# Deformable sampling in a two-layer network: the product with a tap's weights moved from one to two steps behind the tap's transposes

## The chip, the cores and the metric

The kernel runs on one core of one Trainium2 chip. What counts is the device time of one execution in microseconds (us). Three runs of the kernel before took 7668.76, 7659.78 and 7680.08 us; their median is 7668.76 us. A further execution was recorded by the hardware profiler; it took 8447.64 us, and its span, from the first to the last instruction of the program, is 8445.7 us.

## The reference, cut to what matters

The input x has the shape (2, 128, 64, 64): two images, 128 channels, 4096 positions. Two layers follow one another. Layer 0 has a deformable convolution and a mixture of experts (FFN), layer 1 a state-space mixer and another FFN. Only the deformable convolution is touched by the change. It has four branches with kernels of 1x1, 1x1, 3x3 and 7x7, so 1 + 1 + 9 + 49 = 60 taps. For each tap and position an offset and a mask are computed, the image is sampled at the shifted place by bilinear interpolation, and the samples are multiplied with the tap's weights and summed over the taps of the branch:

```python
def deform_conv(x, off_w, off_b, mod_w, mod_b, reg_w, k, pad):
    offset = conv2d(x, off_w, off_b, pad)
    mask = 2.0 * jax.nn.sigmoid(conv2d(x, mod_w, mod_b, pad))
    ...
    py = base_y + off[:, :, 0]
    px = base_x + off[:, :, 1]
    sampled = bilinear_sample(x, py, px) * mask[:, None]
    O = reg_w.shape[0]
    return jnp.einsum('bckhw,ock->bohw', sampled, reg_w.reshape(O, C, k * k))

def branch(x, off_w, off_b, mod_w, mod_b, reg_w, gng, gnb, k, pad):
    y = deform_conv(x, off_w, off_b, mod_w, mod_b, reg_w, k, pad)
    return jax.nn.relu(group_norm(y, gng, gnb))
```

`bilinear_sample` reads four corners around each place and adds them with their weights. Each branch gives 256 channels. The four branches and a fifth, pooled one are joined by a 1x1 convolution with a group norm, and the result is added to x.

## The kernel before, in words

Everything is in fp32. The positions of an image are cut into 8 groups (NG) of 512, that is 4 tiles (GT) of 128 positions. For the sampling, a table in DRAM holds, for each place of the padded image, the four corners' channels beside each other (512 numbers, 2 KB), so that one row fetches all that a sample needs.

`run` works in this order. It normalises image 0 and writes its table. It computes the offsets of the first group. Then it calls `sample` for the 8 groups of image 0, and after that for the 8 groups of image 1: 2 x 8 x 60 = 960 taps.

One tap in `sample` does the following. POOL issues four gathers (L548), one for each tile of 128 positions, into a buffer v of 128 x 4 x 512 numbers; the pool of v has six buffers. DVE multiplies the upper two corners with their weights (L559), and, for two tiles at a time, the lower two into a PSUM tile `low` (L564), and adds them (L565). PE then transposes the two remaining halves of each tile onto each other, eight transposes (L569), into a PSUM tile `pst`, of which there are two. That adds the last two addends and puts the channels on the partitions. ACT copies `pst` into the SBUF tile `st` (L578), of which there are two. PE multiplies the weights of the tap with `st`, once for each half of the 256 output channels (L597), into the two PSUM tiles `out`, which gather all taps of a branch; the profile counts four matmul passes for it.

That product isn't issued in its own tap. `self.late` holds it, and it is issued in the next step, behind the next tap's transposes and copy. So PE's order in the steady state is: transposes of tap k, product of tap k-1, then the side work of the step, then the transposes of tap k+1. `product` also does what hangs on it. When it was the last of ten taps of a chunk of weights, it puts the loading of a later chunk (`load_chunk`, L234, a DMA of 1280 KB on SP's queue) on a list, `self.pending`, to be issued some steps later. When it was the last tap of a branch, ACT copies both tiles `out` to `ys` (L611) and stores them to DRAM (L612), and the statistics of `ys` on DVE (bn_stats) go on the same list.

Each step ends with side work. `conv.step()` issues a piece of the offsets of later groups: seven products (L336), which the profile shows as fourteen matmul passes. `rest.step()`, twice a step and three times in the first group, takes a step of other generators: in image 0 the norm and table of image 1 and the constant matrices of the mixer; in image 1 the generator `after(0)`, which does the end of layer 0's convolution for image 0 (`finish`), its FFN and the convolutions of the mixer. `finish` needs the sums of all branches of its image in DRAM and their statistics. It begins with two DMAs of weights and then yields until `self.pending` is empty.

The order of work on each engine is the order in which these Python functions issue it (`manual_schedule`); nothing is rearranged. Semaphores are set by the framework, and a tile that has all its buffers in use makes the instruction that would write it wait.

After the sampling, `mixer.run` works through the scan of layer 1 for image 0, 256 units, with `after(1)` as side work at four or five steps a unit, and then for image 1. In it POOL does the multiplications `db` (L1239) for the scan, and in the FFN of layer 0 the multiplications `gb` (L806). The FFN of layer 1 comes last.

Of the kernel before, what the change touches and what calls it, by code (L numbers as in the profile page):

```python
# [9 lines left out]
F32 = mybir.dt.float32  # L10
# [8 lines left out]
P = 128  # L19
# [9 lines left out]
NG = NT // GT  # L29
BRANCH = [(1, 0), (1, 0), (3, 1), (7, 3)]  # L30
TAPS = [(j, ky, kx, p) for j, (k, p) in enumerate(BRANCH) for ky in range(k) for kx in range(k)]
NTAP = len(TAPS)
# [139 lines left out]
def together(gens, n):  # L172
    for _ in mixed(gens, n):
        pass


class L0Conv:
# [281 lines left out]
    def run(self, build, after):  # L459

        env, tc, nc = self.env, self.env.tc, self.env.nc
        pools = lambda ctx: lambda name, bufs, **kw: ctx.enter_context(tc.tile_pool(name=name, bufs=bufs, **kw))
        with ExitStack() as ctx:
            pool = pools(ctx)
            self.rp, self.regw = pool("l0rw", 1), {}
            self.ip = pool("l0i", 2)
            self.vp = pool("l0v", 6)
            self.stp = pool("l0s", 2)
            self.pending = []
            first = ctx.enter_context(ExitStack())  # L470
            self.open_offsets(pools(first))
            for i in range(2):
                nc.vector.memset(self.padc[i], 0.0)
            self.zero_table(0)
            with (
                tc.tile_pool(name="nrm", bufs=3) as sp,
                tc.tile_pool(name="nrmp", bufs=4, space=PSUM) as pp,
            ):
                together([self.norm_group(0, g, sp, pp, "nrm") for g in range(NG)], 3)
            self.load_weights()  # L480
            self.zero_table(1)
            for _ in self.norm_end(0):
                pass
            self.p_w = pool("l0pw", 1, space=PSUM)
            self.p_r = pool("l0pr", 1, space=PSUM)
            self.p_t = pool("l0pt", 2, space=PSUM)
            self.p_o = pool("l0py", 2, space=PSUM)
            psum = ctx.enter_context(ExitStack())
            self.p_f = deque([pools(psum)("l0po", 1, space=PSUM)])
            early = psum.enter_context(ExitStack())  # L490
            p_m = pools(early)("l0pm", 1, space=PSUM)

            def more():

                early.close()
                self.p_f.append(pools(psum)("l0po2", 1, space=PSUM))
                yield

            cur = self.new_group(self.ip)
            for _ in self.offset_stream([(0, 0, cur)]):  # L500
                pass

            conv, rest = Side(), Side()
            self.late = None
            rest.add(self.norm(1, p_m, "misc"), more(), build)
            ahead = {}

            def runs():
                for g in range(1, NG):
                    ahead[g] = self.new_group(self.ip)  # L510
                    yield 0, g, ahead[g]
                    yield 1, g - 1, None
                yield 1, NG - 1, None

            conv.add(self.offset_stream(runs()))
            for g in range(NG):
                self.sample(0, g, *cur, conv, rest, 2 if g else 3)
                cur = ahead.get(g + 1)
            conv.drain()
            rest.drain()  # L520
            psum.close()
            first.close()
            side = ctx.enter_context(tc.tile_pool(name="l0ps", bufs=2, space=PSUM))
            rest.add(after(0, side))
            cur = self.load_group(1, 0)
            for g in range(NG):
                nxt = self.load_group(1, g + 1) if g + 1 < NG else None
                self.sample(1, g, *cur, conv, rest, 2 if g else 3)
                cur = nxt
            self.late()  # L530
            for _, f in self.pending:
                f()
            self.pending = []
            rest.drain()

    def sample(self, b, g, idx, w4, conv, rest, pace):

        env, nc = self.env, self.env.nc
        pw = None
        for br, (k, _) in enumerate(BRANCH):  # L540
            for t in range(FIRST[br], FIRST[br] + k * k):
                tw = t % HT
                if tw == 0:
                    pw = self.p_w.tile([P, GT, HT, 4], F32, name="pw")
                    nc.vector.tensor_copy(pw, w4[:, :, t : t + HT, :])
                v = self.vp.tile([P, GT, 4 * C], F32, name="v")
                for j in range(GT):
                    nc.gpsimd.indirect_dma_start(  # L548
                        out=v[:, j, :],
                        out_offset=None,  # L550
                        in_=self.table[b],
                        in_offset=bass.IndirectOffsetOnAxis(ap=idx[:, j, t : t + 1], axis=0),
                    )
                v4 = v.rearrange("p j (q c) -> p j q c", q=4)


                up = v4[:, :, 0:2, :]
                w = pw[:, :, tw, 0:2].unsqueeze(3).to_broadcast([P, GT, 2, C])
                nc.vector.tensor_tensor(up, up, w, ALU.mult)  # L559
                for j in range(0, GT, 2):  # L560
                    two = slice(j, j + 2)
                    low = self.p_r.tile([P, 2, 2, C], F32, name="low")
                    w = pw[:, two, tw, 2:4].unsqueeze(3).to_broadcast([P, 2, 2, C])
                    nc.vector.tensor_tensor(low, v4[:, two, 2:4, :], w, ALU.mult)  # L564
                    nc.vector.tensor_tensor(up[:, two], up[:, two], low, ALU.add)  # L565
                pt = self.p_t.tile([P, GT, P], F32, name="pst")
                for j in range(GT):
                    for q in range(2):
                        nc.tensor.matmul(  # L569
                            pt[:, j, :],  # L570
                            v4[:, j, q, :],
                            env.ident,
                            is_transpose=True,
                            start=j == 0 and q == 0,
                            stop=j == GT - 1 and q == 1,
                        )
                st = self.stp.tile([P, 512], F32, name="st")
                nc.scalar.copy(st, pt.rearrange("p j t -> p (j t)"))  # L578
                if self.late:
                    self.late()  # L580
                self.late = functools.partial(self.product, b, g, br, t, st)
                due = [f for n, f in self.pending if n == 0]
                self.pending = [(n - 1, f) for n, f in self.pending if n]
                for f in due:
                    f()
                conv.step()
                for _ in range(pace):
                    rest.step()

    def product(self, b, g, br, t, st):  # L590

        nc = self.env.nc
        first, last = t == FIRST[br], t == FIRST[br] + BRANCH[br][0] ** 2 - 1
        if first:
            self.out = [self.p_o.tile([P, 512], F32, name="out") for _ in range(2)]
        for half in range(2):
            nc.tensor.matmul(  # L597
                self.out[half],
                self.regw[t // CH][:, t % CH, half * P : (half + 1) * P],
                st,  # L600
                start=first,
                stop=last,
            )
        c = t // CH
        if t % CH == CH - 1 and c in (0, 1, 3, 4) and not (b == B - 1 and g == NG - 1 and c > 2):
            self.pending.append((4, functools.partial(self.load_chunk, c + 3 if c < 3 else c - 3)))
        if last:
            for half in range(2):
                r = 2 * br + half
                ys = self.stp.tile([P, 512], F32, name="ys", bufs=4)  # L610
                nc.scalar.copy(ys, self.out[half])  # L611
                nc.scalar.dma_start(out=self.yd[b][r, :, g * 512 : (g + 1) * 512], in_=ys)  # L612
                self.pending.append((4, functools.partial(nc.vector.bn_stats, self.stats[b][:, r, g, :], ys)))

    def finish(self, b, fp, sp, pp, cs):
# [8 lines left out]
        nc.sync.dma_start(out=pw, in_=d["pool_w"])  # L624
        mv = fp.tile([P, 10, 2], F32, name="mv")

        for _ in range(2):
            yield
        while self.pending:
            yield  # L630
        for i in range(8):
            nc.vector.bn_aggr(mv[:, i, :], stats[:, i, :, :])
# [1001 lines left out]
```

## Time and profile before

| | |
|---|---|
| median of three runs | 7668.76 us (7659.78 to 7680.08) |
| the profiled execution | 8447.64 us |
| its span | 8445.7 us |
| first and last gather (L548) | 199.0 and 6010.5 us |
| first and last product of the sampling (L597) | 241.0 and 6025.7 us |
| granted TensorE clock, mean of the span | 0.798 |
| DMA, mean over the span | 186 GB/s |

The profiled execution is longer than the timed ones by 778.88 us, so its durations can't simply be set against the median. In a row of the page's groups, the numbers before the bar say how often the group ran; behind it stand its busy time in us, the mean of one in ns, and the idle time of its engine just before it, with what ended the largest part of that. "remote" means that a semaphore ended the wait for which the profile could name no instruction. In a timeline row the first number is the start, the second the duration, both in us, and the brackets hold the idle time of the engine before it. The rows on PE come in two kinds: PE are matmuls, PEld the loading of weights ahead of them. The ends of matmuls are modelled by the profiler.

### The profile page before, as it was taken

The page shows a single profiled execution, that of the slowest core. Times are in us where ns is not written, and L with a number is a line of the kernel's source. Part 1 is how long each engine was busy: PE and PEld are TensorE (multiplying, and loading weights), DVE is VectorE, ACT ScalarE, POOL GpSimd, SP SyncE. Part 2 cuts the span into 40 slices and gives each one's busy share as a digit, 9 for nine tenths or more (in the row PEclk, how much of TensorE's full clock was granted, in tenths as well). Part 3 has the DMA queues.
Part 4 walks back from the last instruction along what each step waited for, and adds up shares of the span by engine and source line. Part 5 has one row for each costly group of instructions (what it writes and reads, how often), then busy time and mean ns, then how long its engine had stood idle before and what let it go on. Part 6 is the DMA issues. An engine that isn't in the chain of part 4 may idle for free. (4 is left out here: it accounts for less than half of the span.)

```text
span 8445.7 us, 85253 instructions
## 1 busy us (share of the span) xinstructions
PE 5931.0 (70%) x28533; PEld 4163.4 (49%) x28533; DVE 5703.1 (68%) x8472; ACT 2111.4 (25%) x4445; POOL 4585.4 (54%) x4556
## 2 busy tenths in 40 slices
PE   2688888888888867677667675667555666645569
PEld 2456566666666634344334443445344555523359
DVE  1577777777777776788876667667557636679950
ACT  1111111111111114111112111212353444555520
POOL 0456666666666666666665666666534323367610
PEclk9789999999999989888878887888776656656555
DMA  4676666666666678777677777777553334333333
GB/s 126 187 256 209 203 200 212 197 211 198 203 213 193 214 220 270 248 233 238 219 233 203 214 227 214 214 213 207 165 170 120 118 88 132 94 120 135 123 96 120
DMA packets 655029, 1574.34 MB, mean 186 GB/s; under 512 B 167768, under 2 KB 280192, under 8 KB 642052
## 3 DMA queue, kind: packets, MB, share of 16 engines
q0 software_dynamic: 307200, 1006.88, 39.8%
q1 hardware_dynamic: 284452, 494.19, 18.4%
q10 hardware_dynamic: 62944, 67.83, 2.3%
q8 instruction: 232, 3.80, 0.2%
q14 instruction: 201, 1.65, 0.1%
HBM read 1450.99 MB, written 120.01 MB: 186 GB/s over the span
## 5 line engine op out<-in xcount | busy, mean ns | idle before, releaser
L548 POOL DMA_INDIRECT v<-table,idx x3840 | 3643.1, 949 | 2367.9 <-issue 990.9
L597 PE MATMUL out<-st,regw 128*128 128x512 f32 x3840 | 2191.6, 700 | 704.2 <-issue 356.4
L559 DVE TENSOR_TENSOR v<-v,pw 128x1024 f32<-128x1024 f32 x960 | 1169.2, 1218 | 1069.9 <-DMA v<-table,idx 911.7
L578 ACT COPY st<-pst 128x512 f32<-128x512 f32 x960 | 557.6, 585 | 4338.7 <-remote 2312.1
L569 PE MATMUL pst<-ident,v 128*128 128x128 f32 x7680 | 1175.2, 296 | 389.3 <-issue 303.5
L597 PEld LDWEIGHTS out<-st,regw 128*128 128x128 f32 x3840 | 765.2, 222 | 1364.5 <-issue 980.4
L565 DVE TENSOR_TENSOR v<-v,low 128x512 f32<-128x512 f32 x1920 | 1318.0, 686 | 67.0 <-issue 1.7
L564 DVE TENSOR_TENSOR low<-v,pw 128x512 f32<-128x512 f32 x1920 | 1328.8, 692 | 34.1 <-DVE v L565 0.7
L569 PEld LDWEIGHTS pst<-ident,v 128*128 128x128 f32 x7680 | 976.4, 153 | 699.6 <-issue 569.0
L1239 POOL TENSOR_TENSOR db<-du,bcb 128x512 f32<-128x512 f32 x512 | 659.7, 1293 | 942.0 <-DVE da L1289 864.7
L336 PEld LDWEIGHTS po<-wout,ring 128*128 128x128 f32 x5120 | 732.6, 198 | 285.5 <-issue 284.5
L336 PE MATMUL po<-wout,ring 128*128 128x147 f32 x5120 | 757.3, 296 | 102.3 <-issue 99.0
L1289 DVE TENSOR_TENSOR_SCAN da<-da,state,db 128x512 f32<-128x512 f32 x512 | 656.9, 1283 | 245.3 <-ACT state L1296 211.4
L1262 PE MATMUL py<-ident,sc 128*128 128x128 f32 x2048 | 480.1, 389 | 374.5 <-DVE sc L1295 374.2
L1262 PEld LDWEIGHTS py<-ident,sc 128*128 128x128 f32 x2048 | 349.7, 201 | 523.2 <-DVE sc L1295 483.1
L1295 DVE TENSOR_TENSOR sc<-da,bcb 128x512 f32<-128x512 f32 x512 | 354.2, 692 | 88.5 <-PE py L1262 42.2
L1246 ACT ACTIVATE da<-delta,w_A_log 128x512 f32<-128x512 f32 x512 | 352.2, 688 | 15.9 <-DVE delta L1209 3.1
L972 PEld LDWEIGHTS ps<-tm,X 120*88 120x88 f32 x2048 | 249.3, 220 | 81.2 <-ACT Y L924 42.0
L972 PE MATMUL ps<-tm,X 120*88 120x48 f32 x2048 | 252.4, 304 | 52.2 <-ACT Y L924 25.8
L1296 ACT COPY state<-da 128x1 f32<-128x1 f32 x512 | 80.4, 157 | 544.6 <-DVE sc L1295 544.0
L988 PE MATMUL ps<-ident,Y 88*64 88x88 f32 x768 | 107.0, 287 | 151.8 <-ACT img L924 92.6
L959 PE MATMUL ps<-ident,hs 64*120 64x64 f32 x1408 | 141.8, 275 | 87.2 <-ACT X L924 75.5
(268 smaller groups left out, 5103.1 us busy)
## 6 DMA issues: line engine op xcount, KB each, us to landing
bcb<-bc SPq DMA_DIRECT2D x256, 512.0 KB
regw<-in_regw SPq DMA_DIRECT2D x66, 1280.0 KB
v<-table,idx POOLq DMA_INDIRECT x3840
yd<-ys ACTq DMA_DIRECT2D x128, 256.0 KB
yc<-yd SPq DMA_DIRECT2D x32, 1024.0 KB
gb<-gd SPq DMA_DIRECT2D x16, 2048.0 KB
tm<-pos SPq DMA_DIRECT2D x16, 1440.0 KB
table<-xn SPq DMA_DIRECT2D x128, 128.0 KB
```

The costliest lines, as they stand in the source:

```text
L336: m()
L548: nc.gpsimd.indirect_dma_start(out=v[:, j, :], out_offset=None, in_=self.table[b], in_offset=bass.IndirectOffsetOnAxis(ap=idx[:, j, t : t ...
L559: nc.vector.tensor_tensor(up, up, w, ALU.mult)
L564: nc.vector.tensor_tensor(low, v4[:, two, 2:4, :], w, ALU.mult)
L565: nc.vector.tensor_tensor(up[:, two], up[:, two], low, ALU.add)
L569: nc.tensor.matmul(pt[:, j, :], v4[:, j, q, :], env.ident, is_transpose=True, start=j == 0 and q == 0, stop=j == GT - 1 and q == 1,)
L578: nc.scalar.copy(st, pt.rearrange("p j t -> p (j t)"))
L597: nc.tensor.matmul(self.out[half], self.regw[t // CH][:, t % CH, half * P : (half + 1) * P], st, start=first, stop=last,)
L972: nc.tensor.matmul(ps[:, c, :], X[:, c0 + c, :], tm[:, :, c0 + c], start=True, stop=True)
L1239: nc.gpsimd.tensor_tensor(dbs[u], pieces[k]["du"][:, half, :], bcb[u // 2][:, 0, :], ALU.mult)
L1262: nc.tensor.matmul(out[:, j, :], what[:, j * P : (j + 1) * P], env.ident, is_transpose=True, start=first and j == 0, stop=last and j == GT ...
L1289: nc.vector.tensor_tensor_scan(s, s, dbs.pop(u), state[:, half, n : n + 1], ALU.mult, ALU.add)
```

## The change

The single delayed product becomes a queue of delayed products. Each step appends its own product, and when more than two wait, the oldest is issued. In the steady state the product of tap k-2 is thus issued behind the transposes of tap k. The tile `st` has three buffers instead of two, since the copies of three taps can be alive at a time. At the end of image 1, whatever is left in the queue is issued. `product` counts the products issued for each image in `self.made`. `finish` yields until all 480 products of its image were issued and `self.pending` is empty, instead of yielding twice and then until the list is empty.

```diff
@@ run
             conv, rest = Side(), Side()
-            self.late = None
+            self.late, self.made = deque(), [0, 0]
@@ run, behind the last tap
-            self.late()
+            for f in self.late:
+                f()
@@ sample
-                st = self.stp.tile([P, 512], F32, name="st")
+                st = self.stp.tile([P, 512], F32, name="st", bufs=3)
                 nc.scalar.copy(st, pt.rearrange("p j t -> p (j t)"))
-                if self.late:
-                    self.late()
-                self.late = functools.partial(self.product, b, g, br, t, st)
+                self.late.append(functools.partial(self.product, b, g, br, t, st))
+                if len(self.late) > 2:
+                    self.late.popleft()()
@@ product
         nc = self.env.nc
+        self.made[b] += 1
@@ finish
-        for _ in range(2):
-            yield
-        while self.pending:
+        while self.made[b] < NG * NTAP or self.pending:
             yield
```

The lines of the code behind the change move: the transposes are L570, the copy L579 and the product L599 in the changed kernel, the gathers L549.

## The prediction

> **What bounds the kernel now.** I read the page first: its span, its engine totals and its groups.
>
> ```profile
> span 8445.7 us, 85253 instructions
> ...
> PE 5931.0 (70%) x28533; PEld 4163.4 (49%) x28533; DVE 5703.1 (68%) x8472; ACT 2111.4 (25%) x4445; POOL 4585.4 (54%) x4556
> ...
> L548 POOL DMA_INDIRECT v<-table,idx x3840 | 3643.1, 949 | 2367.9 <-issue 990.9
> L597 PE MATMUL out<-st,regw 128*128 128x512 f32 x3840 | 2191.6, 700 | 704.2 <-issue 356.4
> ...
> L578 ACT COPY st<-pst 128x512 f32<-128x512 f32 x960 | 557.6, 585 | 4338.7 <-remote 2312.1
> ```
>
> No engine is full over the span, so the stage must be taken alone. The rows of tile v put the first gather at 199.0 us and the last at 6010.5: 5811.5 us for 960 taps, 6.05 each, 69% of the span. The other 30% (the mixer and the last FFN) is touched only at one seam.
>
> In this stage POOL issues four gathers a tap. The timeline spaces them 1.25 us apart when nothing holds them (0.95 busy, 0.30 issue), so POOL alone needs 3643.1 + 3840 x 0.30 = 4795 us. The remaining 1017 us are waits of POOL. The windows of L548 show 212 gathers in the first 600 us: 600 - 199 - 212 x 1.25 = 136 us of the waits lie there. The other 881 spread over 907 taps, 0.97 each. The waits say for whom:
>
> ```profile
> POOL v L548 <- issue: 990.9, 3244, 0.6
> POOL v L548 <- remote: 458.5, 187, 4.7
> POOL v L548 <- PE pst L569: 391.8, 162, 12.4
> ```
>
> "issue" is the floor above; the two other rows are POOL waiting for a buffer v, which the transposes L569 free. The timeline shows why the transposes are late (PE and ACT rows):
>
> ```profile
> 1514.57 1.04 PE L569 MATMUL pst<-ident,v 128*128 128x128 f32 x8
> 1515.44 1.88 PE L597 MATMUL out<-st,regw 128*128 128x512 f32 x4
> 1517.16 1.93 PE L336 MATMUL po<-wout,ring 128*128 128x147 f32 x14
> 1518.93 1.03 PE L569 MATMUL pst<-ident,v 128*128 128x128 f32 x8
> 1519.80 1.88 PE L597 MATMUL out<-st,regw 128*128 128x512 f32 x4
> 1521.52 1.93 PE L336 MATMUL po<-wout,ring 128*128 128x147 f32 x14
> 1523.28 0.98 PE L569 MATMUL pst<-ident,v 128*128 128x128 f32 x5
> 1524.70 0.54 PE L569 MATMUL pst<-ident,v 128*128 128x128 f32 x3 [0.44 <-issue]
> ...
> 1526.24 0.58 ACT L578 COPY st<-pst 128x512 f32<-128x512 f32 x1 [8.13 <-PE pst L569]
> 1526.43 0.94 POOL L548 DMA_INDIRECT v<-table,idx  x1 [1.85 <-PE pst L569]
> ...
> 1526.88 1.99 PE L597 MATMUL out<-st,regw 128*128 128x512 f32 x4 [1.64 <-issue]
> ```
>
> Unhindered, PE needs 4.36 us a tap for the first image (1514.57 to 1518.93), less than POOL's 5.0. But the product of 1526.88 needs the copy of 1526.24, the copy of the transposes that ended at 1519.96. That copy came 6.3 us after them, ACT idle before it. PE stood 1.64 us, and POOL was released in the same moment. So PE, which has the work of 4.36 us, is held by a copy that is late, and POOL by PE.
>
> **The profiled execution is not the timed one.** It took 8447.64 us (1.94 around its span), the median of the runs is 7668.76: 778.88 less. If head (199) and tail (8445.7 - 6010.5 = 2435) cost the same in both, the gathers take 7668.76 - 199 - 2435 - 2 = 5033 us there, 238 above POOL's 4795. Most of the 1017 us of waits would then not exist when nothing is recorded. This decides the forecast.
>
> [...] granted clock 0.50 from 1501 to 1507, 1.00 from 1508 to 1524, 0.91 over 600 to 3100 and 0.84 over 3100 to 6030. [...]
>
> **The change, part by part.**
> - *Product two taps behind.* PE's row becomes: transposes of tap k, product of k-2, offset matmuls or side steps. No instruction is added or removed. Between the end of tap k's transposes and the first instruction that needs its copy lay, unhindered, 1515.61 to 1519.80 = 4.2 us (its product). Now that first instruction is the transposes of k+2, since pst keeps two buffers: 1515.61 to 1523.28 = 7.7 us. The wait moves from the product to these transposes; behind it stand that tap's product and side matmuls, and DVE and ACT wait for the latter. The copy needed there is one tap older than the one that stopped PE before, so no transpose waits longer than now. Cost zero, gain from zero up to all waits behind a late copy.
> - *Third st.* The copy of k must find the product of k-3 done; with two buffers and the old order it was k-2. Either stands before tap k's transposes on PE: 0. It adds 2 KB a partition.
> - *Drain of the queue.* The last two products run after the last tap, four passes of 0.43 us instead of none: +1.7 us. At the first image's end two products run inside the second image, hidden under POOL's 5.0 us a tap.
> - *One tap later:* ys copies with their yd DMAs on ACT's queue, bn_stats on DVE, and load_chunk with its DMA on SP's queue (past up to three side steps' DMAs). A chunk still is asked for five taps after its predecessor's last product and needed some 15 taps (75 us) later: 0. Uncovered, it would hold a product and one tap, 5 us, 66 times.
> - *finish waits for a count.* For the first image it starts about one tap (two or three side steps) later. Its chain ends before the sampling does (no side row stands in 6009 to 6026 of the timeline): 0. For the second image the two empty yields fall away, so its chain moves two steps forward against the mixer's scan, which takes four or five steps a unit. POOL's order there changes: gb (L806, 8 x 4.73 us) meets other neighbours.
>
> The sum on the profiled execution: from 0 to -881 us (+1.7). On the timed one the gather stage has only 238 us above its floor. If the first 600 us keep their 136 (the norm of the second image shares the DMA queues there, and DVE waits for landings), 102 are left. I take half of them, since side chains also hold DVE (19.4 us at 5017.95, for xst), where a later product helps nothing: **-50 us, 7620**. Both ends: 0, and 238 as long as a gather costs 1.25.
>
> **Rivals.**
> - *Modest gain, as worked out: 7620, own range 7555 to 7646. Chance 0.45.* For it: PE's waits before L597, 704 us, the largest of its groups. Against: the copy may not be late at all without the recorder.
> - *No change: 7669, within 23 us. 0.20.* POOL already runs at 5.03 to 5.24 us a tap in the timed runs, and the six v buffers (six taps, 30 us) swallow what PE loses. For it: the 778.88 us.
> - *Large gain: 7420. 0.20.* The recorder slows everything alike (7668.76 / 8447.64 = 0.908). The gathers then take 5276 of a floor of 4353, so 923 us of waits are real; a quarter to a third of them gone is -250. For it: POOL waits much alike in both images, by the windows of L548 0.89 us a tap over 600 to 3100 and 1.06 over 3100 to 6030. Against: the gathers' 0.95 us is so even that I doubt that recording lengthens it.
> - *Slower: 7715. 0.15.* The seam in the mixer: with the second image's chain two steps earlier, gb comes to stand before the multiplications db (L1239) at points where the scan has no lead. Lead is three units, 1987 / 512 x 3 = 11.6 us; a db behind two xs or zc (1.3 to 2.2 each) and two gb (9.5) is past it. Eight gb wholly exposed are 38 us; I take 46, for what then waits on ACT and PE behind them. For it: POOL idles 864.7 us for da there, so the scan is a strict alternation; against: the same idle time is its slack.
>
> **How the numbers follow.** A measurement of this kernel tells about 0.3% (23 us) from no change. Faster: 0.45 + 0.20 = 0.65; same 0.20; slower 0.15. The likeliest case gives 7620. The range leaves out the lower half of the large gain (0.10, below 7420) and two thirds of the slower case (0.10, above 7710): 7420 to 7710.
>
> **What would show it.** Right: in the changed kernel's trace the group L599 has far less than 704 us of idle before it, part of it back before L570 with ACT st as releaser; the granted clock over 600 to 3100 above 0.91; POOL's waits for pst and "remote" below 850 together, the gathers still 1.25 apart. Wrong in size: if the profiled span falls by hundreds of us while the timed runs fall by 50 or less, the recorder had made the lateness; if the timed runs fall by more than 238, a gather costs less than 1.25 unrecorded or my head and tail do. Wrong in place: if the copies come as late as before, now one tap further on (about 7.7 us after the transposes), the signal was waiting for PE to stop, and no distance helps. Slower: the stretch after the last gather over 2435 us.

## The result, and the profile after

The changed kernel takes 7717.85 us (median of 6 runs, 7709.35 to 7738.3) where the kernel before takes 7672.42 (6 runs beside it, 7659.78 to 7681.92): ratio 1.0063, 95% interval 1.0046 to 1.008. It is slower by some 45 us, and the forecast was 7620. One thing is needed to read the numbers: the second batch of experiments (e5 to e8) ran on a chip on which the kernel before takes about 8385 us, where others take 7651 to 7672, so every experiment is compared with the kernel before on its own chip. The execution that was profiled first, of 8447.64 us, resembles those of that chip; whether it ran there isn't known. In the text TensorE is PE, VectorE DVE, ScalarE ACT, GpSimd POOL and SyncE SP.

The page of the changed kernel, with the lines that answer to those shown of before:

```profile
span 7707.6 us, 85112 instructions
...
PE 5671.2 (74%) x28533; PEld 3994.3 (52%) x28533; DVE 5681.0 (74%) x8472; ACT 2121.9 (28%) x4441; POOL 4593.8 (60%) x4556
...
L549 POOL DMA_INDIRECT v<-table,idx x3840 | 3651.1, 951 | 1588.3 <-issue 937.2
L599 PE MATMUL out<-st,regw 128*128 128x512 f32 x3840 | 1994.9, 646 | 51.6 <-ACT ys L613 51.6
L579 ACT COPY st<-pst 128x512 f32<-128x512 f32 x960 | 562.4, 586 | 3500.7 <-PE pst L570 3470.5
...
L1295 DVE TENSOR_TENSOR sc<-da,bcb 128x512 f32<-128x512 f32 x512 | 354.2, 692 | 112.6 <-PE py L1262 65.2
```

The idle time before the product (L599) is 51.6 us, and the profiled execution is 738 us shorter than that of before. Read against the first profile, this looks like the gain that was forecast. It is not. The kernel before, profiled once more (the run `e3_before_again`, 7657.45 us), has the same lines without the change:

```profile
span 7655.5 us, 85253 instructions
...
L548 POOL DMA_INDIRECT v<-table,idx x3840 | 3641.8, 948 | 1582.3 <-issue 928.6
L597 PE MATMUL out<-st,regw 128*128 128x512 f32 x3840 | 1989.8, 644 | 55.4 <-ACT ys L611 53.5
...
L1295 DVE TENSOR_TENSOR sc<-da,bcb 128x512 f32<-128x512 f32 x512 | 354.2, 692 | 85.9 <-PE py L1262 39.4
```

Its product waited 55.4 us, not 704.2. POOL's waits are alike too. First the changed kernel, then the kernel before, in the view of waits (us in total, times, longest):

```profile
POOL v L549 <- issue: 937.2, 3068, 1.6
POOL v L549 <- PE pst L570: 178.2, 103, 7.7
POOL v L549 <- DMA v<-table,idx: 127.3, 309, 4.2
```

```profile
POOL v L548 <- issue: 928.6, 3047, 0.6
POOL v L548 <- PE pst L569: 170.4, 103, 7.5
POOL v L548 <- DMA v<-table,idx: 135.8, 333, 5.8
```

The timeline of the kernel before shows a tap as it is where nothing is late (rows of PE and ACT, two taps):

```profile
1516.39 1.04 PE L569 MATMUL pst<-ident,v 128*128 128x128 f32 x8
1517.26 1.88 PE L597 MATMUL out<-st,regw 128*128 128x512 f32 x4
1517.52 0.58 ACT L578 COPY st<-pst 128x512 f32<-128x512 f32 x1 [3.77 <-PE pst L569]
...
1518.98 1.93 PE L336 MATMUL po<-wout,ring 128*128 128x147 f32 x14
...
1520.74 1.03 PE L569 MATMUL pst<-ident,v 128*128 128x128 f32 x8
...
1521.62 1.88 PE L597 MATMUL out<-st,regw 128*128 128x512 f32 x4
```

The copy starts at 1517.52, 0.09 us after the transposes end, and is done at 1518.10, 3.5 us before its product at 1521.62. The median over all 960 taps is the same 0.09 us, so a product one tap behind has its operand in time already. The 6.3 us that the prediction read between the transposes and a copy are therefore no distance that belongs to the program.

From the starts of the gathers, taps 60 to 540 take 5.035 us each in both: 599.6 to 3016.3 us in the changed kernel, 606.4 to 3023.2 in the kernel before. The difference of the spans, 52.1 us, lies elsewhere: 17.3 us at the end of the last product (5252.6 against 5235.3) and 34.8 us in the stretch from there to the end, here called the tail (2455.0 against 2420.2). Of the 17.3, the taps 540 to 660 alone lose 22.4 (675.6 against 653.2 us); 6.8 were gained ahead of tap 60. Each of these stretches is read from one recorded execution, and the tails of kernels with all gathers and the side chain of before range from 2412 to 2423 us. So there are two places, and in neither is the product concerned.

### The profile page after: what moved, and what is told of

Its sections match the earlier page's. It is cut to its first block, busy times and chain, and to the rows that moved or that the text cites. A ratio compares the mean times of both kernels' runs of the same rounds, so it can differ in the third digit from the quotient of the medians.

```text
span 7707.6 us, 85112 instructions
## 1 busy us (share of the span) xinstructions
PE 5671.2 (74%) x28533; PEld 3994.3 (52%) x28533; DVE 5681.0 (74%) x8472; ACT 2121.9 (28%) x4441; POOL 4593.8 (60%) x4556
## 5 line engine op out<-in xcount | busy, mean ns | idle before, releaser
L549 POOL DMA_INDIRECT v<-table,idx x3840 | 3651.1, 951 | 1588.3 <-issue 937.2
L599 PE MATMUL out<-st,regw 128*128 128x512 f32 x3840 | 1994.9, 646 | 51.6 <-ACT ys L613 51.6
L570 PE MATMUL pst<-ident,v 128*128 128x128 f32 x7680 | 1201.1, 293 | 743.3 <-issue 420.2
L579 ACT COPY st<-pst 128x512 f32<-128x512 f32 x960 | 562.4, 586 | 3500.7 <-PE pst L570 3470.5
L570 PEld LDWEIGHTS pst<-ident,v 128*128 128x128 f32 x7680 | 918.0, 149 | 1149.3 <-issue 674.6
L599 PEld LDWEIGHTS out<-st,regw 128*128 128x128 f32 x3840 | 722.6, 209 | 586.1 <-issue 520.6
L336 PEld LDWEIGHTS po<-wout,ring 128*128 128x128 f32 x5120 | 693.0, 190 | 150.6 <-issue 150.6
L336 PE MATMUL po<-wout,ring 128*128 128x147 f32 x5120 | 706.5, 288 | 0.0
L972 PEld LDWEIGHTS ps<-tm,X 120*88 120x88 f32 x2048 | 246.9, 216 | 62.1 <-issue 37.3
L675 PE MATMUL pfo<-yc,fw 128*128 128x256 f32 x512 | 149.4, 442 | 56.4 <-ACT yc L677 56.4
```

What stands on the lines that cost most here:

```text
L336: m()
L549: nc.gpsimd.indirect_dma_start(out=v[:, j, :], out_offset=None, in_=self.table[b], in_offset=bass.IndirectOffsetOnAxis(ap=idx[:, j, t : t ...
L570: nc.tensor.matmul(pt[:, j, :], v4[:, j, q, :], env.ident, is_transpose=True, start=j == 0 and q == 0, stop=j == GT - 1 and q == 1,)
L599: nc.tensor.matmul(self.out[half], self.regw[t // CH][:, t % CH, half * P : (half + 1) * P], st, start=first, stop=last,)
L972: nc.tensor.matmul(ps[:, c, :], X[:, c0 + c, :], tm[:, :, c0 + c], start=True, stop=True)
```

## The experiments

Two things happen at these places. From about tap 490 on the first image's finish runs as side steps, and in taps 540 to 660 the feed-forward that follows it (FFN; its multiplications gb fall in taps 561 to 645). The change starts this side chain one tap later, since the last product, its statistics and the count come one tap later. In the mixer the second image's finish starts two side steps sooner, since two empty yields were dropped.

**Which part costs.** First the two yields put back into the changed kernel, and the same two taken out of the kernel before, for the second image alone:

```diff
 changed kernel, finish (e1)
+        for _ in range(2):
+            yield
         while self.made[b] < NG * NTAP or self.pending:
 kernel before, finish (e2)
-        for _ in range(2):
+        for _ in range(0 if b else 2):
             yield
```

> The changed kernel with the two empty yields put back in front of the wait in finish, so that the second image's side chain meets the mixer's scan where it did before; queue, third st and count stay. Seam theory (the loss lies in the mixer, because the chain starts two side steps earlier): the stretch from the last product to the end goes back from 2455 to about 2419 us, and the time to 7665 to 7690. Queue theory (the loss lies in the sampling): the stretch may move, the time stays at 7705 to 7735.

> The kernel before with nothing changed but the two empty yields in finish, left out for the second image. Seam theory: 7700 to 7725, 30 to 50 us slower than before, with ACT waiting some 16 times for pfo in the mixer. Queue theory: within 10 us of before.

Measured: with the yields back 7671.17 against 7653.56, ratio 1.0023 (1.0013 to 1.0033); the tail is 2422.1. The kernel before without them: 7697.7, ratio 1.0067 (1.0051 to 1.0082); tail 2461.0. Two empty yields, which issue nothing, are worth more than 40 us, and without any later product. What remains of the change costs 0.0023: a share of the time of the kernel before, as all such figures below, about 18 us.

The kernel before once more, and with a third buffer for st alone, first in a single run and then timed:

```diff
-                st = self.stp.tile([P, 512], F32, name="st")
+                st = self.stp.tile([P, 512], F32, name="st", bufs=3)
```

> The kernel before, profiled a second time. If the late copies belong to this program under the recorder, its profiled span is again near 8446 us, copies 3 to 8 us behind their transposes. If the first profile was an accident, the span is near 7670 and copies follow within 0.1 us.

> The kernel before with three buffers of st and nothing else. If the third buffer removes the late copies from the profile, its span is near 7670; if the order on PE does, near 8446 as before. The time without a profile stays within 15 us of before under either.

> The kernel before with a third buffer for the copied samples and nothing else, timed. If a copy sometimes waits for the product of two taps earlier, the single look (7646) stands: ratio 0.998 to 0.9995. If the buffer is never waited for, 0.9995 to 1.0005.

The first gave the profile shown above: the late copies don't belong to the program. The buffer gave 7646.36 in the single run and a ratio of 1.0009 (0.9999 to 1.0018) when timed: above both ranges expected, but no effect that can be told from none.

**The remaining 0.0023: the later product, or the side chain that it shifts?** One run keeps the later product and lets the deferred statistics and chunk loads fall due one tap earlier, so that VectorE, GpSimd and SyncE issue exactly what the kernel before issues; the other has the kernel before and only shifts the first image's side chain by a tap.

```diff
 changed kernel with its two yields back, product (e5)
-                self.pending.append((4, functools.partial(nc.vector.bn_stats, ...)))
+                self.pending.append((3, functools.partial(nc.vector.bn_stats, ...)))
 (the same 3 for load_chunk)
 kernel before, finish (e6)
         while self.pending:
             yield
+        for _ in range(0 if b else 3):
+            yield
```

> The changed kernel with the two empty yields back and with the deferred statistics due after 3 taps instead of 4, so that VectorE, GpSimd and SyncE issue exactly what they issue in the kernel before, in the same order; only the product and the copies of finished sums stand one tap later on TensorE and ScalarE. Theory A (what is left of the loss, about 17 us of 7653, comes from the side chain of the first image, which starts one tap later): ratio 0.999 to 1.001, taps 540 to 660 at the pace of the kernel before (5.35 and 5.54 us a tap). Theory B (the later product itself costs it, by standing in TensorE's queue ahead of side work): ratio 1.002 as with the yields alone, taps 540 to 600 at 5.5 us or more.

> The kernel before, with three yields after the finish's wait for the first image, which is one tap at the pace of that group; no queue, two buffers. Theory A: the loss is here, ratio 1.0015 to 1.003, taps 540 to 600 at 5.5 us. Theory B: nothing changes, 0.999 to 1.001.

Measured against 8385.15: the later product alone 8384.64, ratio 0.9997 (0.9987 to 1.0007); the shifted side chain alone 8401.55, ratio 1.0022 (1.0014 to 1.003). The second is as large as the whole remainder. (The paces expected in microseconds a tap were those of a chip at 7650 us and don't apply here. With the later product the taps 540 to 600 and 600 to 660 take 5.93 and 5.92 us each, with the shifted chain 6.11 and 6.12.)

This chip also has the late copies that the prediction was built on, so it answers the forecast on its own ground. The two runs' rows for product and transposes, first the kernel before with the shifted chain, then that with the later product:

```profile
L597 PE MATMUL out<-st,regw 128*128 128x512 f32 x3840 | 2165.2, 692 | 626.5 <-issue 321.4
...
L569 PE MATMUL pst<-ident,v 128*128 128x128 f32 x7680 | 1182.3, 299 | 358.5 <-issue 289.3
```

```profile
L599 PE MATMUL out<-st,regw 128*128 128x512 f32 x3840 | 2080.3, 667 | 117.9 <-issue 97.4
...
L570 PE MATMUL pst<-ident,v 128*128 128x128 f32 x7680 | 1232.0, 305 | 745.2 <-issue 491.7
```

The product's idle time falls by 508.6 us and that of the transposes rises by 386.7. In taps 60 to 540 copies come a median 3.60 us after their transposes with the later product and 3.44 without it, and a tap takes 5.82 us against 5.83. Most of the wait was moved, and no time was gained.

The opposite shift of the side chain, statistics and chunk loads due after 3 taps in the kernel before:

```diff
-            self.pending.append((4, ...
+            self.pending.append((3, ...
 (both places, as in e5)
```

> The kernel before with the deferred statistics due after 3 taps instead of 4, so that the first image's finish starts one tap sooner. If a later side chain costs because it is late, sooner gains: 0.997 to 0.999. If it is how its steps fall against the taps, any sign can come; a repeated loss (1.001 to 1.003) or no change would speak for it.

Ratio 1.0007 (0.9997 to 1.0017), not told from none. In its trace taps 540 to 660 take 670.0 us, where a run of the same batch with the side chain of before (e10, below) takes 654.0. In that one execution a tap sooner costs there what a tap later costs (671.1 with the yields back), though the medians show no loss of that size in the whole, and where it is made up isn't known. This speaks for how side steps and taps fall together, and against mere lateness; it doesn't prove it. VectorE has little room in this stretch. The kernel before and then the changed kernel with its yields back, over these 120 taps (window, length; busy us of PE, PEld, DVE, ACT, POOL; granted clock, DMA share, GB/s), each with its longest differing wait:

```profile
3023.20:3676.40 653.20, 481.91 (x2156) 292.99 (x2156) 571.93 (x932) 108.55 (x189) 461.08 (x481) 0.91 0.79 255
DVE gb L808 <- DMA gb<-gd: 16.4, 8, 4.9
```

```profile
3017.80:3688.90 671.10, 488.06 (x2164) 292.98 (x2164) 572.55 (x926) 108.76 (x188) 460.79 (x481) 0.89 0.77 250
DVE gb L810 <- DMA gb<-gd: 24.8, 8, 6.0
```

VectorE does 572 us of work in either and is 88% busy in the first. The 18 us are more waiting: 8.4 for the loads of gb (an input of the FFN), and 2 to 3 each in other short waits (for lg, hs, n_st and v). No one wait stands for them all.

**Where in the mixer the two yields go.** The finish makes one group of 256 columns in five side steps: matmuls into the PSUM tile pfo, the activation fa (L685) on ScalarE that copies it, and the statistics fst of fa on VectorE. The scan takes five side steps a unit, so one group falls on each unit, at a fixed place within it. Without the yields fa came in the same unit as the matmuls pfo that it reads, and ScalarE waited for them 16 times of 16. If that were the cause, a shift by five would leave it:

```diff
 changed kernel, finish (e7)
+        for _ in range(5):
+            yield
         while self.made[b] < NG * NTAP or self.pending:
```

> The changed kernel with five yields before the finish's wait; the first image's finish isn't moved by them, the second image's starts one whole unit of the scan later than without any. Phase theory (the finish has five yields a group of columns and the scan takes five steps a unit, so a shift by five leaves each activation where it is within its unit): as slow as the changed kernel, ratio 1.005 to 1.008, tail from the last product to the end about 2455 us. Delay theory (what the two yields gave was time, and five give more): 1.002 or less, tail 2422 us or less.

Ratio 1.0022 (1.0013 to 1.0031), which is the first image's part alone; the tail is 2408.0, against 2412.4 to 2422.9 for the three runs beside it. The phase theory, which expected the whole loss, falls: the same place within a unit doesn't give the same time. The delay theory's tail came true, and its ratio within the interval. ScalarE did wait for pfo 16 times (22.2 us), and the sixteenth unit of the scan (its operation da on VectorE) began 131.6 us after the last product, against 126.1 to 128.7 in the runs beside it, but by the forty-ninth unit it was ahead (299.2 against 303.2 to 304.4). Of the 256 units of an image the first 192 take five steps and the last 64 four; the units that won time back lie among the 192, so this doesn't explain it.

So the two were parted: fa moved two side steps later for the second image, in the changed kernel; and the kernel before with five yields and that.

```diff
-            fa = sp.tile([P, 512], F32, name="fa", bufs=2)
-            nc.scalar.activation(fa[:, :cs], po, AF.Identity, bias=fv)
-            ...
+            late.append(close)      # the same lines; called at i == 3 of the next group
+            if not b:
+                late.pop()()
```

> The changed kernel, with the second image's activation fa (and its store) issued two side steps after the matmuls pfo that it reads, instead of in the next step; nothing else moved. If what costs the changed kernel time in the mixer is ScalarE standing at fa for the matmul of the same unit, the sixteenth unit of the scan starts about 90 us after the last product, as in the kernel before, instead of 116, and of the 35 us of the tail 20 to 28 come back: ratio 1.002 to 1.004 (the first image's 0.002 stays). If it is the alignment of the rest of the side chain, the unit starts at 110 or later and the ratio stays 1.005 to 1.008.

> The kernel before with five yields ahead of the second image's finish instead of two and its activation fa two side steps later. The first image and the sampling are as in the kernel before. From the run with five yields (tail 2408 against 2418 to 2423 of its neighbours, though its first sixteen units took 13 us more) and the activation's theory: the tail falls to 2395 to 2405, ratio 0.997 to 0.9985. If the activation isn't the cause: tail 2408 to 2412, 0.9985 to 0.9995.

The first: 7699.23 against 7661.57, ratio 1.0053 (1.0037 to 1.0069), tail 2445.4, within the range of the second theory. The wait for pfo is all but gone from the mixer (0.8 us) and the sixteen activations take 106 us from the first to the last instead of 119, yet most of the loss stays. (The expectation's 90 and 116 us for the sixteenth unit don't come out of the traces by the count used above: it starts at 129.9 in the kernel before, at 137.3 in the changed one and at 134.6 here.) The second: ratio 0.9991 (0.9984 to 0.9999), tail 2417.7. That ratio is in the range expected if the activation isn't the cause, and the tail is within the range of the kernel before; the expectation had left out a neighbour of 2412.4. It is the fastest of the timed versions that leave nothing out, and by less than a measurement of this kernel tells.

Then the empty steps were put behind the finish, so that the finish is as in the changed kernel and the feed-forward behind it as in the kernel before, without and with the later fa, beside the changed kernel on one chip:

```diff
 changed kernel, end of finish (e14; e13 has the later fa too)
         yield from mixed([residual(g) for g in range(NG)], 2)
+        for _ in range(2 if b else 0):
+            yield
```

> The changed kernel itself, timed beside the two that follow, so that they can be compared on one chip: 1.005 to 1.0075, tail from the last product to the end 2450 to 2460 us.

> The changed kernel with two empty side steps after the second image's finish instead of before its wait, so that all that follows the finish (the groups of the feed-forward) falls against the scan's units as in the kernel before, and the finish itself as in the changed one. If the loss of the tail lies in the finish alone, it stays: 1.005 or more, tail 2450. If most of it lies in what follows (of the 35 us, 10 went when only the activation was moved), 1.003 to 1.0045, tail 2428 to 2436.

> Both: the activation fa of the second image two steps later, and the two empty steps after its finish. If these two are the whole of the seam, the tail is 2416 to 2424 and the ratio 1.0015 to 1.003, that of the run with the two yields back, which is the first image's part. If something else is in it, the ratio stays above 1.0035.

| kernel | median us (before 7650.94) | ratio, 95% interval | tail us, one execution |
|---|---|---|---|
| changed (e15) | 7704.89 | 1.0068, 1.0055 to 1.0081 | 2446.9 |
| two steps after the finish (e14) | 7684.9 | 1.0037, 1.0024 to 1.005 | 2430.4 |
| the same and fa later (e13) | 7664.26 | 1.0017, 1.0011 to 1.0024 | 2417.8 |

All three fell as the theory of two places said: the two steps behind the finish bring 0.0031, the later fa 0.0020, and 0.0017 is left for the first image. VectorE's waits change with both. Here sc is the scan's product on VectorE, which TensorE adds up into py. Whole-span rows of the changed kernel (e15), of e14, and of e13, in this order:

```profile
DVE sc L1295 <- PE py L1262: 64.6, 25, 10.8
DVE fst L683 <- ACT fa L685: 97.4, 24, 8.4
ACT fa L685 <- PE pfo L675: 43.2, 26, 2.5
```

```profile
DVE sc L1297 <- PE py L1264: 42.0, 26, 8.3
DVE fst L683 <- ACT fa L685: 113.5, 24, 8.5
ACT fa L685 <- PE pfo L675: 43.7, 26, 2.8
```

```profile
DVE sc L1309 <- PE py L1276: 41.1, 25, 8.3
DVE fst L685 <- ACT fa L689: 96.0, 24, 11.6
ACT fa L689 <- PE pfo L675: 19.4, 10, 2.0
```

With two steps behind the finish, the scan's product sc waits 22.6 us less for TensorE's py, which shares PE with the feed-forward's matmuls; the kernel before has 39.4 in that row. With the later fa, VectorE's bn_stats waits 17.5 less for fa, and ScalarE 24.3 less for pfo. These rows take in both images. Behind the last product, where only the second image's finish runs, the waits of fst for fa sum to 74.7, 75.2 and 62.1 us in these three kernels and to 55.6 in the kernel before.

These rows go with the loss, but they don't prove its path. The run with five yields (e7) has nearly the rows of the changed kernel and a tail of 2408.0:

```profile
DVE sc L1297 <- PE py L1264: 61.8, 23, 10.9
DVE fst L685 <- ACT fa L687: 93.6, 22, 8.6
```

What makes up for them there was not followed. So the experiments show which steps cost and how much; which wait carries the loss to the end stays open.

**Would the later product pay anywhere?** Three runs leave work out. In the first, 24 of every 49 matmuls of the offset convolution are missing (the expectation says 25, but the edit keeps the 25 even ones), and with them part of TensorE's load in the first image; the gathers then also read other rows of the table. In the others two of the four gathers of each tap are missing, without and with the later product (side chain as in the kernel before).

```diff
 e12
-                    for m in mats[7 * i : 7 * i + 7]:
+                    for m in mats[7 * i : 7 * i + 7][i % 2 :: 2]:
 e16, e17 (v from six buffers that are written once at the start)
-                for j in range(GT):
+                for j in range(0, GT, 2):
                     nc.gpsimd.indirect_dma_start(
```

> The kernel before with 25 of each 49 matmuls of the offset convolution (the even ones) left out, 1.6 matmuls a tap in taps 60 to 420; the offsets are then not the reference's. On a chip where the gathers keep their 5.01 us a tap nothing changes there (5.00 to 5.02). On a chip like the one of the first profile and of the second batch (5.82 us a tap) two theories part: TensorE's own work is the bound there, then 5.2 to 5.4 us a tap; the wait is a late signal or a slow transfer, then 5.75 to 5.85.

> The kernel before with two of the four gathers of each tap left out (the other half of the samples is what the buffers held, so the output is not the reference's); GpSimd's floor falls from 5.01 to about 2.5 us a tap. TensorE's recorded work is 4.5 us a tap in taps 60 to 540, VectorE's 4.3. If the product of the kernel before still has its copy early when the gathers bind nothing, a tap takes 4.5 to 4.7 us; if it then waits for the copy, 4.8 or more.

> The same with the product two taps behind and the third buffer, all other engines as in the run beside it. Theory A (the later product pays once the gathers are no longer the bound): 0.1 us a tap or more less than beside it, 50 to 250 us of the whole. Theory B (its copy was never late on a sound chip): within 0.03 us a tap of it, 15 us of the whole.

Without the matmuls, on a chip at 7661.57, the taps 60 to 480 keep their 5.02 us (570.5 to 2678.3) while TensorE's busy time in them falls from 1886 (e10) to 1648 us, so TensorE binds nothing there; the whole is 40 us shorter (one run, 7621.98), nearly all of it ahead of tap 60, which starts at 570.5 us instead of 608.6 (e10). The question for the chip of 8385 us stays open, since this run was not on it.

With half of the gathers: 7101.6, ratio 0.9283 (0.9267 to 0.9299); with the later product as well 7090.45, ratio 0.9269 (0.9253 to 0.9284). Their windows over 600 to 2700 us, columns as above, first without and then with the later product:

```profile
600.00:2700.00 2100.00, 2000.96 (x11128) 1492.17 (x11125) 2014.22 (x3190) 514.83 (x1178) 903.36 (x952) 0.99 0.55 166
```

```profile
600.00:2700.00 2100.00, 1999.71 (x11111) 1484.04 (x11109) 2009.13 (x3183) 514.56 (x1177) 898.76 (x951) 1.00 0.55 165
```

Over taps 60 to 540 a tap takes 4.41 us without and 4.42 with the later product, less than either theory of e16 expected, with TensorE and VectorE at 95 to 96%. Even where the gathers no longer bind, the product one tap behind loses nothing to its copy (a median 0.09 us behind its transposes); theory A, which expected 50 us or more, falls: the medians differ by 11 us, and the intervals overlap.

## Why the prediction was wrong

Three parts of the prediction failed. The product two taps behind was to gain 50 us and gained nothing. The later start of the first image's finish was put at 0 and costs about 17 us. The two yields that fall away for the second image were left out of the sum, and without them it takes about 40 us more. The first alone would have left the time where it was; the other two made it longer.

- **The view that it was built on was of another regime.** The prediction read a wait of 704 us before the product and copies 6.3 us late from one execution of 8447.64 us, and saw that the timed runs were 779 us shorter. It drew the right conclusion ("most of the 1017 us of waits would then not exist") and then did not use it on the mechanism itself: it still took half of the 102 us that it thought remained. In the regime that was timed the copy is 0.09 us behind its transposes and the product's wait is 55.4 us, of which 53.5 stand for ys, not st. The term was -50; measured, no change (0.9997, 0.9987 to 1.0007), and that on the chip where copies are late.
- **The floor was right.** Gathers 1.25 us apart: 5.035 us a tap in both kernels, and half of the gathers took 7% off the whole. It booked half of the 102 us above the floor as gain and doubted the rest, since side chains also hold VectorE. In the second profile some 110 us lie above 5.01 us a tap behind tap 60, and all of them behind tap 480, where the side chains of the first image run: the changed kernel has no fewer of them (from tap 480 to the last tap 2527.0 us against 2509.4), so none was the product's to win.
- **The cause that it considered, recording, is not shown.** That recording makes the difference of 778.88 us was an assumption of its author. Recorded executions elsewhere stand by the unrecorded ones: 7657.45 beside 7653.56, and 8385.36 beside 8384.64. Executions of about the first profile's length came again on one chip, recorded (8385.36) or not (8367.72 to 8411.2).
- **"Wrong in place" came true in part, where it could be seen.** The prediction said that if copies come as late with one tap more of distance, no distance helps. On the chip with late copies no time was gained, and most of the wait went from L597 to L570, the place that the prediction had named for it. But the copies came no later than before, 3.60 us after their transposes against 3.44, not 7.7, so the reason given (the signal waits for PE to stop) isn't shown.
- **"finish waits for a count ... 0" for the first image** is the first of the steps put at nothing that failed. The reason given, that this chain ends before the sampling does, is true and not enough. In taps 540 to 660 the chain shares VectorE with the sampling; starting it one tap later costs 16 to 18 us, 0.0022.
- **The two empty yields of the second image** were seen, but only as a rival with a chance of 0.15, and were left out of the sum. They are about 0.005 of the 0.0068. The rival had the right place, but its number, 7715, is close to the measured 7718 by luck: its mechanism was gb on GpSimd delaying the multiplications db, and it knew of no loss in the first image. In the whole mixer VectorE's scan waited for db 7.8 us, twice, in the kernel before and just as long in the changed one. The waits that grew are ScalarE's for pfo, that of VectorE's statistics for fa, and that of sc for TensorE; the run with five yields has them too without the loss, so they are named here as company, not as the cause.
- **Third buffer, drain of the queue, chunk loads one tap later:** costed at 0, 1.7 and 0. The buffer alone shows no effect (1.0009, 0.9999 to 1.0018), and the run with the later product alone shows none of the drain, which at 1.7 us is smaller than it can tell.

What stays open: why one chip takes 5.8 us a tap with late copies; which of the many short waits in taps 540 to 660 comes first; and why five steps more in the mixer cost nothing where none do. That the side chain's start is the cause was shown by shifting it alone; how it comes to cost time was not followed wait by wait.

## What to carry to other kernels

Before a wait is priced, make sure that the profiled execution is one of those that are timed; if its time is off by a tenth, the waits in it may be none of theirs, and a second profile costs little. When side work is advanced a fixed number of steps per unit of the main loop, an edit that adds or drops steps (even empty ones) or delays the condition on which it starts moves everything behind it against that loop, so it must be costed as a change of its own, at every place where the two share a busy engine. Here a dependency that was one iteration deep and already early gained nothing from a second iteration, and none where it was late either.

## What was not expected of the hardware

The kernel before, one program, has medians of 7650.94 to 7672.42 us in five batches and of 8385.15 in one (59 runs there, 8367.72 to 8411.2). The difference lies almost wholly in the sampling: the tail is 2417.7 us there, in the run with the later product, against 2420.2 of the kernel before elsewhere. Over 240 taps of the first image, the kernel before at 7657 us, and the later product alone at 8385 us:

```profile
907.20:2109.50 1202.30, 1090.70 (x6026) 813.76 (x6025) 1034.62 (x1642) 234.56 (x569) 909.68 (x961) 0.97 0.79 240
```

```profile
1001.00:2396.70 1395.70, 1189.25 (x6025) 884.35 (x6024) 1041.27 (x1641) 233.89 (x568) 912.19 (x961) 0.91 0.68 207
```

For as many instructions VectorE, ScalarE and GpSimd are busy as long as elsewhere (within 0.7%), TensorE 9% longer, at a granted clock of 0.91 instead of 0.97, and the stretch takes 193 us more. The clock's share can't be told from these rows, since TensorE also has more gaps: 206 us of the stretch without recorded work, against 112. It is 85% busy at the clock of 0.91 and 91% busy at 0.97; in the runs with half of the gathers it is 95% busy, at 0.99 and 1.00. So a slower clock may be the reason for the longer stretch or its result; these runs don't show which.
